# Two layers on one core: attention scores held one head to a PSUM bank, and expert gates spread by transfers

## Chip, cores and metric

One core of a Trainium2 chip runs the whole program. The metric is the device time in microseconds (us) of one execution; before the change it is 1755.88 us, the median of three runs (1743.19 to 1758.93).

The engines are named as in the profile: PE multiplies matrices (PEld is its weight load), DVE is the vector engine, ACT evaluates functions, POOL is the third elementwise engine, SP issues most transfers. PE writes to PSUM, here eight banks of 128 partitions by 512 float32 each. DVE and ACT read the banks and so free them.

## What is computed

2048 tokens of width 128 pass through two layers, each with two parts that are added to the residual stream x:

```python
x = x + ssd(layernorm(x))                  # layer 0: state-space mixer, 8 heads, state 16
h = layernorm(x)                           # layer 0, second part
h1 = h + causal_attention(layernorm(h))    # 16 heads of width 8, all 2048 keys
x = x + h1 + experts(layernorm(h1))        # 8 experts of 128 x 512 x 128, the best 2 gated
x = x + scan(layernorm(x))                 # layer 1: selective scan, 256 channels, state 16
x = x + feed(layernorm(x))                 # layer 1: 128 -> 512 -> 512 -> 512 -> 128

# the attention
scores = where(causal, q @ k.T / sqrt(8), lowest)     # per head, 2048 x 2048
out = softmax(scores) @ v
# the experts
moe_out = sum(gate[:, e] * (gelu(x @ fc1[e] + b1[e]) @ fc2[e] + b2[e]) for e in range(8))
```

## The kernel before

**Tiles.** The tokens are four chunks c of 512 (C). Every part works on a chunk: `ssd(c)`, `prepare(c)` (layernorm, q, k and v), the attention of the chunk, `conclude(c)`, `experts(c)`, `scan(c)`, `feed(c)`. The 16 heads are four groups g of four heads, and the four heads of a group lie on four partition strips of 32, so a score product of one head uses one strip of 32 rows of PE ("32*128" in the profile). The pair (c, g) is one job of the attention, 16 in all.

**The attention of a job has two passes.** `shift(c, g)` (lines 287 to 325) finds for every query the largest score: for each 128 queries r and each chunk of keys kc it multiplies q by k (line 302) for two heads into the two banks of one tile `ps_m`, adds the causal mask with a 128 x 128 product where the keys are the chunk's own (line 311), and one DVE reduction takes the maximum of both heads (line 312). Its result `sh` is laid out at lines 316 to 324. `weighted(c, g)` (lines 327 to 384) goes over the 128-key blocks kb: for two heads at a time it multiplies k by q (line 352) into the two banks of one tile `ps_e`, adds the shift of each query by a second product (line 358), adds the mask on the diagonal (line 360), and one ACT exponential of both heads writes `probs` (line 362). `sum_up` (lines 334 to 342) then multiplies the values by `probs` of all four heads into `ps_o` (line 339, four products on four strips of columns, "128*9"). It is called for block kb - 1 after the first pair of block kb, and the first two of the four products are made to wait for the last exponential of their block as well. A score tile is 2 banks deep and has one buffer, so the next pair's line 302 waits for line 312, and the next pair's line 352 waits for line 362.

**What sets the order.** All parts are Python generators which yield the cost of what they have just written. `in_step` writes a step of `weighted(c, g)` beside steps of `shift` of the next job; `with_attention` writes so much attention between two yields of the other parts (`state_spaces` first, then `second_layers`) as RATE says. The layer above then orders the instructions of each engine by their readiness and by this written order, and puts in the semaphores. Each engine runs its own list strictly in order. After the attention has ended, `scan(2)` with `experts(3)`, `scan(3)` with `feed(2)`, and `feed(3)` alone make up the tail (lines 973 to 978).

**Banks.** `BUFS` at line 81 deals the eight: `m` one tile of two banks, `e` one tile of two banks, `o` one, `a` two, `c` one. The other parts take `a` for their products and `c` for their sums (`Stream`, lines 657 to 688); `ssd` takes `a` and `c` while attention runs beside it. In the tail the stream `other` turns round `m` and `e` and sums in `o` (line 974). The helper `whole` (line 141) hands out half of an `m` or `e` tile where a part asks for one bank.

**Gates.** `experts` (lines 722 to 804) computes the gate of each token and expert, transposes them to rows in `gT` (lines 757 to 774, with a second product that splits them in two halves of precision), and for each expert one product with a selecting weight (`spread_row`, line 719) writes the expert's row to all 128 partitions of a bank; line 785 copies it to `gb`, and line 796 multiplies the expert's output by it. The scan spreads its rows of B in another way: they are written to a DRAM scratch (line 840) and read back to all partitions, one row a transfer of 256 KB (line 861, `bb`).

## Time and profile before

| | us |
|---|---|
| median of three runs (lowest, highest) | 1755.88 (1743.19, 1758.93) |
| the profiled execution | 1741.55 |
| its span, first to last instruction | 1739.8 |
| PE busy, by the page | 1466.9 |
| DVE busy, ACT busy | 975.0, 726.2 |
| mean granted PE clock | 0.837 of full |
| `ssd(0)` alone | about 0 to 140 |
| attention beside the other parts | about 140 to 1410 |
| tail | about 1410 to 1740 |

The page gives busy time by engine, the span in 40 slices (busy tenths, and in the row PEclk the granted PE clock in tenths), and groups of instructions with their count, their busy time and the mean of one. Busy time of a group is the time in which at least one of its instructions ran, so that 640 products of 0.52 us which run two or four abreast are busy for less than their sum. "Idle before" is the engine's idle time just before instructions of the group, with what ended it. The waits view sums the same by who waited for whom. The timeline lists instructions by their start.

### The profile page before, as it was taken

Reading aid. Unit: us, or ns where it says so; the run is one execution under the profiler, and the core shown is the slowest. Engines: PE = TensorE matmul, PEld = TensorE weight load, DVE = VectorE, ACT = ScalarE, POOL = GpSimd, SP = SyncE. Lnnn points to the kernel's source line nnn. Section 1 sums busy time; section 2 is a strip of 40 time slices with the busy share of each in tenths; the row PEclk is TensorE's granted clock in tenths of the full one; section 3 lists DMA queues with packets and bytes.
Section 4 is the critical chain, followed back from the end, with each engine's and each line's share of the span. In section 5 each row is a group of like instructions: output and inputs, shape, how many; then the busy total and the mean of one; then the engine's idle time right before and its main releaser. Section 6 shows DMA issues by size and latency. Waiting matters only on the chain. (4 is left out here: it accounts for less than half of the span.)

```text
span 1739.8 us, 16427 instructions
## 1 busy us (share of the span) xinstructions
PE 1466.9 (84%) x6306; PEld 633.5 (36%) x6306; DVE 975.0 (56%) x1556; ACT 726.2 (42%) x847; POOL 284.0 (16%) x316
## 2 busy tenths in 40 slices
PE   6898999998999888888978887789999888658528
PEld 3554545444333333232333322433333233223214
DVE  4566646557344565667466686674442036774950
ACT  2222322322445444555354454355563536534522
POOL 3322210211000100112111021110000001440220
PEclk9898997887899978889677898669996899868859
DMA  2000000001000000324220045320011022860841
GB/s 85 1 1 1 1 1 1 1 1 55 24 25 25 25 13 21 83 49 103 55 49 14 30 99 107 68 42 25 24 37 31 24 67 78 178 125 31 188 96 30
DMA packets 62494, 83.24 MB, mean 48 GB/s; under 512 B 4576, under 2 KB 28816, under 8 KB 62416
## 3 DMA queue, kind: packets, MB, share of 16 engines
q0 software_dynamic: 16320, 31.46, 10.4%
q1 hardware_dynamic: 45664, 49.68, 9.7%
q8 instruction: 49, 0.80, 0.2%
q10 hardware_dynamic: 432, 1.06, 0.2%
q14 instruction: 29, 0.24, 0.0%
HBM read 49.55 MB, written 1.18 MB: 29 GB/s over the span
## 5 line engine op out<-in xcount | busy, mean ns | idle before, releaser
L362 ACT ACTIVATE probs<-ps_e 128x1024 f32<-128x1024 f32 (+3 forms) x320 | 286.6, 896 | 505.8 <-PE ps_e L358 304.0
L312 DVE TENSOR_REDUCE top<-ps_m 128x2 f32<-128x1024 f32 (+3 forms) x320 | 339.7, 1062 | 280.8 <-PE ps_m L302 164.1
L302 PE MATMUL ps_m<-kR,qR 32*128 32x512 f32 (+3 forms) x640 | 190.1, 523 | 68.0 <-DVE top L312 55.2
L352 PE MATMUL ps_e<-qR,kR 32*128 32x512 f32 (+3 forms) x640 | 175.5, 519 | 27.5 <-ACT probs L362 26.8
L339 PE MATMUL ps_o<-probs,vv 128*9 128x512 f32 (+3 forms) x1152 | 169.7, 599 | 1.0 <-ACT probs L362 0.9
L302 PEld LDWEIGHTS ps_m<-kR,qR 32*128 32x128 f32 x640 | 78.6, 208 | 242.9 <-DVE top L312 132.1
L867 DVE TENSOR_TENSOR_SCAN db<-da,hlast,db 128x512 f32<-128x512 f32 x128 | 163.0, 1310 | 6.5 <-ACT da L863 4.7
L358 PE MATMUL ps_e<-sh,onesR 32*128 32x512 f32 (+3 forms) x640 | 148.9, 431 | 0.0
L352 PEld LDWEIGHTS ps_e<-qR,kR 32*128 32x128 f32 x640 | 69.7, 204 | 182.0 <-ACT probs L362 106.3
L789 PE MATMUL ps_a<-nT,wide 128*128 128x512 f32 x192 | 113.8, 699 | 6.0 <-ACT h L790 3.7
L794 PE MATMUL ps_c<-h,wide 128*128 128x512 f32 x192 | 103.5, 643 | 0.0
L798 POOL TENSOR_TENSOR acc<-acc,ye 128x512 f32<-128x512 f32 x28 | 43.6, 1558 | 331.5 <-DVE ye L796 331.5
L871 POOL COPY hlast<-db 128x2 f32<-128x2 f32 x48 | 29.4, 612 | 378.9 <-DVE db L867 378.9
L863 ACT ACTIVATE da<-dl 128x1024 f32<-128x1024 f32 x64 | 66.4, 1054 | 51.5 <-DMA db<-db 28.3
L865 DVE TENSOR_TENSOR db<-du,bb 128x1024 f32<-128x1024 f32 x64 | 77.9, 1227 | 16.3 <-issue 11.0
L790 ACT ACTIVATE h<-ps_a,cols 128x512 f32<-128x512 f32 x96 | 63.8, 686 | 52.2 <-PE ps_a L789 51.9
L358 PEld LDWEIGHTS ps_e<-sh,onesR 32*128 32x128 f32 x640 | 77.2, 219 | 3.2 <-issue 1.8
L927 PE MATMUL ps_a<-g,wide 128*128 128x512 f32 x96 | 54.0, 690 | 19.5 <-ACT g L930 19.5
L789 PEld LDWEIGHTS ps_a<-nT,wide 128*128 128x128 f32 x192 | 37.1, 215 | 46.3 <-issue 19.5
L362 ACT ACT_TABLE_LOAD x41 | 52.6, 1283 | 1.3 <-PE ps_e L358 0.6
L927 PE MATMUL ps_a<-h,wide 128*128 128x512 f32 x96 | 51.1, 665 | 0.8 <-ACT g L930 0.8
L375 DVE COPY os<-ps_o 128x512 f32<-128x512 f32 x16 | 10.9, 684 | 70.8 <-PE ps_o L339 70.7
(375 smaller groups left out, 2129.3 us busy)
## 6 DMA issues: line engine op xcount, KB each, us to landing
wide<-in_fc SPq DMA_DIRECT2D x64, 256.0 KB, 3.2
bb<-scratch_b SPq DMA_DIRECT2D x64, 256.0 KB, 3.5
db<-db POOLq DMA_DIRECT2D x32, 512.0 KB, 5.7
u<-db POOLq DMA_DIRECT2D x28, 512.0 KB, 6.0
wide<-in_h SPq DMA_DIRECT2D x16, 512.0 KB, 3.7
wide<-in_w SPq DMA_DIRECT2D x8, 256.0 KB, 3.1
x<-in_x SPq DMA_DIRECT2D x4, 256.0 KB, 5.1
w<-in_w SPq DMA_DIRECT2D x4, 256.0 KB, 4.0
```

The source lines that it names most:

```text
L302: nc.tensor.matmul(pss[:, j, 0:n], qR[hr, w - P : w], kR[hr, g, kc * C : kc * C + n], start=True, stop=not diag,)
L312: nc.vector.tensor_reduce(top[:, i : i + 2, kc], pss[:, :, 0:n], AX.X, ALU.max)
L339: pv = nc.tensor.matmul(o, v, prs[i // 2][:, i % 2, q0:], start=kb == 0, stop=kb == nk - 1)
L352: nc.tensor.matmul(pss[:, j, q0:], kR[hr, g, kb * P : (kb + 1) * P], qR[hr, q0:], start=True, stop=False)
L358: nc.tensor.matmul(pss[:, j, q0:], onesR[hr], sh[hr, q0:], start=False, stop=not diag)
L362: last = nc.scalar.activation(pr[:, :, q0:], pss[:, :, q0:], AF.Exp, scale=float(1.0 / np.sqrt(np.float32(HD))))
L789: nc.tensor.matmul(ph, we[:, 0, f * P : (f + 1) * P], nT, start=True, stop=True)
L794: nc.tensor.matmul(py, we[:, 1, f * P : (f + 1) * P], hs[f // 2][:, f % 2, :], start=f == 0, stop=f == NF - 1)
L863: in_turn("exp", nc.scalar.activation(da, dl, AF.Exp, scale=-float(n + 1)))
L865: nc.vector.tensor_tensor(db, du, bb.unsqueeze(1).to_broadcast(two), ALU.mult)
L867: nc.vector.tensor_tensor_scan(db[:, j, :], da[:, j, :], db[:, j, :], hlast[:, j, n : n + 1], ALU.mult, ALU.add)
L927: nc.tensor.matmul(ph, w[k // 2][:, k % 2, f * P : (f + 1) * P], h[k // 2][:, k % 2, :], start=k == 0, stop=k == NF - 1)
```

## The change

One head's scores take one bank. `m` has two buffers of one bank, `e` three; `c` is gone, and what used it takes `a` or the tags listed below. `shift` goes head by head in the order 2, 3, 0, 1. In `weighted`, head i's scores are written and the head is kept in `begun`; at the next head, `finish` adds its shift and mask and issues its exponential just before the next head's scores are written. `probs` remains a tile of two heads. `sum_up` of block kb - 1 comes after the second head of block kb. The gates are transposed once, written to a DRAM scratch and read back, one row a transfer to 128 partitions, in SP's queue. B is no longer held twice (48 rows become 32). The diff, cut to its core:

```diff
-    BUFS = {"m": 1, "e": 1, "o": 1, "a": 2, "c": 1}
+    BUFS = {"m": 2, "e": 3, "o": 1, "a": 2}
...
# prepare: q and k
-                pf = psum("m" if n == "k" else "e", [P, 2, C])
                 for j in range(2):
-                    nc.tensor.matmul(pf[:, j], w[:, g + j], nT, start=True, stop=True)
+                    pf = psum("m" if n == "k" else "e", [P, C])
+                    nc.tensor.matmul(pf, w[:, g + j], nT, start=True, stop=True)
...
# shift
-                for i in (2, 0):
-                    pss = psum("m", [P, 2, C])
-                    for j in range(2):
-                        hr = slice(32 * (i + j), 32 * (i + j) + 32)
-                        nc.tensor.matmul(
-                            pss[:, j, 0:n],
-                            qR[hr, w - P : w],
-                            kR[hr, g, kc * C : kc * C + n],
-                            start=True,
-                            stop=not diag,
-                        )
+                for i in (2, 3, 0, 1):
+                    hr = slice(32 * i, 32 * i + 32)
+                    pss = psum("m", [P, C])
+                    nc.tensor.matmul(
+                        pss[:, 0:n], qR[hr, w - P : w], kR[hr, g, kc * C : kc * C + n], start=True, stop=not diag
+                    )
                     yield None
-                    for j in range(2 * diag):
-                        nc.tensor.matmul(pss[:, j, w - P : w], ident16, mask_qk, start=False, stop=True)
-                    nc.vector.tensor_reduce(top[:, i : i + 2, kc], pss[:, :, 0:n], AX.X, ALU.max)
-                    yield 0.4
+                    if diag:
+                        nc.tensor.matmul(pss[:, w - P : w], ident16, mask_qk, start=False, stop=True)
+                    nc.vector.tensor_reduce(top[:, i, kc : kc + 1], pss[:, 0:n], AX.X, ALU.max)
+                    yield 0.2
...
# weighted
+        def finish(kb, diag, q0, i, pss, pr):
+            hr = slice(32 * i, 32 * i + 32)
+            nc.tensor.matmul(pss[:, q0:], onesR[hr], sh[hr, q0:], start=False, stop=not diag)
+            if diag:
+                nc.tensor.matmul(pss[:, q0 : q0 + P], ident16, mask_kq, start=False, stop=True)
+            last = nc.scalar.activation(
+                pr[:, i % 2, q0:], pss[:, q0:], AF.Exp, scale=float(1.0 / np.sqrt(np.float32(HD)))
+            )
+            return in_turn("exp", last)
+
+        begun = None
...
-            for i in range(0, 4, 2):
-                pss = psum("e", [P, 2, C])
...
+            for i in range(4):
+                hr = slice(32 * i, 32 * i + 32)
+                if i % 2 == 0:
+                    prs.append(ak.tile([P, 2, C], F32, tag="probs", name="probs", bufs=3))
+
+                if begun:
+                    last = finish(*begun)
+                pss = psum("e", [P, C])
+                nc.tensor.matmul(pss[:, q0:], kR[hr, g, kb * P : (kb + 1) * P], qR[hr, q0:], start=True, stop=False)
+                begun = (kb, diag, q0, i, pss, prs[-1])
                 yield None
-                if i == 0 and waiting:
+                if i == 0 and kb:
+                    waiting.append((kb - 1, q_before, prs_before, last))
+                if i == 1 and waiting:
                     sum_up(*waiting.pop())
-                yield 1.1
-            waiting.append((kb, q0, prs, last))
-        sum_up(*waiting.pop())
+                yield 0.55
+            q_before, prs_before = q0, prs
+        last = finish(*begun)
+        sum_up(nk - 1, q0, prs, last)
...
# ssd alone, then ssd beside attention
-        bigs, smalls = ["a", "a", "e"], ["c", "o", "m"]
+        bigs, smalls = ["a", "a", "e", "e"], ["o", "m", "e", "m"]
...
-        bigs[:], smalls[:] = ["a"], ["c"]
+        bigs[:], smalls[:] = ["a"], ["a"]
...
-    side = Stream("", wk, 4, 6, ("a",), "c")
-    scans = Stream("s", wk, 8, 4, ("a",), "c")
+    side = Stream("", wk, 4, 6, ("a",), "a")
+    scans = Stream("s", wk, 8, 4, ("a",), "a")
...
# experts
-        for i in range(2):
-            nc.vector.tensor_tensor(ge2[:, :, i], ge, top.unsqueeze(2).to_broadcast([P, NB, NE]), ALU.mult)
-        pgt = z.bank([2 * NE, C])
...
-        nc.tensor.matmul(pgt, minus_low[NE], ghi, start=False, stop=True, skip_group_check=True)
-        nc.vector.tensor_copy(gT[0 : 2 * NE], pgt)
+        nc.vector.tensor_tensor(ge, ge, top.unsqueeze(2).to_broadcast([P, NB, NE]), ALU.mult)
+        pgt = z.bank([NE, C])
+        for b in range(NB):
+            nc.tensor.transpose(pgt[:, b * P : (b + 1) * P], ge[:, b], ident)
+        gT = z.line("gT", (NE, C))
+        nc.vector.tensor_copy(gT, pgt)
+        gates = scratch_g[c % 2]
+        nc.sync.dma_start(gates, gT)
...
-            pg = z.bank([P, C])
-            spread_row(pg, NE, gT, e)
             gb = z.line("gb")
-            nc.vector.tensor_copy(gb, pg)
+            nc.sync.dma_start(gb, gates[e].partition_broadcast(P))
...
# the tail
-        other = Stream("o", pool, 6, 8, ("m", "e"), "o")
+        other = Stream("o", pool, 6, 8, ("m", "e", "m", "e", "e"), "o")
```

## The prediction on record

> **What bounds the kernel now.** I read the page first: busy times and the slices.
>
> ```profile
> PE 1466.9 (84%) x6306; PEld 633.5 (36%) x6306; DVE 975.0 (56%) x1556; ACT 726.2 (42%) x847; POOL 284.0 (16%) x316
> PE   6898999998999888888978887789999888658528
> PEclk9898997887899978889677898669996899868859
> ```
>
> PE is the fullest engine until the tail, and for long stretches its clock is below full. DVE and ACT have room. So the sum below is one over PE: what it streams, and what it stands still for. Next the page's groups of the attention.
>
> ```profile
> L362 ACT ACTIVATE probs<-ps_e 128x1024 f32<-128x1024 f32 (+3 forms) x320 | 286.6, 896 | 505.8 <-PE ps_e L358 304.0
> L312 DVE TENSOR_REDUCE top<-ps_m 128x2 f32<-128x1024 f32 (+3 forms) x320 | 339.7, 1062 | 280.8 <-PE ps_m L302 164.1
> L302 PE MATMUL ps_m<-kR,qR 32*128 32x512 f32 (+3 forms) x640 | 190.1, 523 | 68.0 <-DVE top L312 55.2
> L352 PE MATMUL ps_e<-qR,kR 32*128 32x512 f32 (+3 forms) x640 | 175.5, 519 | 27.5 <-ACT probs L362 26.8
> ```
>
> 640 products of 0.52 us are busy for only 190 us: heads on different strips run abreast. Then the timeline, in a stretch with no other part beside the attention (the first three lines), and in one with masks (the last four):
>
> ```profile
> 1021.34 0.39 PE L358 MATMUL ps_e<-sh,onesR 32*128 32x512 f32 x2
> 1021.83 1.02 ACT L362 ACTIVATE probs<-ps_e 128x1024 f32<-128x1024 f32 x1 [0.88 <-PE ps_e L358]
> 1022.90 0.51 PE L352 MATMUL ps_e<-qR,kR 32*128 32x512 f32 x2
> ...
> 559.53 0.29 PE L311 MATMUL ps_m<-mask_qk,ident 128*128 128x128 bf16 x2
> 559.75 0.38 PE L352 MATMUL ps_e<-qR,kR 32*128 32x256 f32 x1
> 559.75 0.49 PE L358 MATMUL ps_e<-sh,onesR 32*128 32x256 f32 x2
> 560.18 0.28 PE L360 MATMUL ps_e<-mask_kq,ident 128*128 128x128 bf16 x2
> ```
>
> The first lines are a closed loop. Line 352 starts at 1021.00 (its line is not copied), the shift on the same strips 0.34 later, the exponential 0.49 after that; it takes 1.02, and the next pair's line 352 starts at 1022.90: 1.90 us a pair, while PE streams 0.33 + 0.32, and half of line 339's 0.86 (four strips abreast): 1.09. The rest is the single buffer. Since a record of 0.50 is followed on its strips after 0.33, 0.17 of a record is drain. With that taken off each PE record, the idle time ahead of lines 302 and 352 in the whole trace is 155 us; by the page's records (68.0 + 27.5) it is 95.5.
>
> **Part 1, more buffers: -100 us.** Softmax: three banks, each held for 0.33 + 0.49 + an exponential of 512 columns (0.60, the row of line 362 in the view by shapes) + 0.1, so a head each 0.5 us; ACT itself needs 0.60. Maxima: a reduction of 512 columns is 0.69 in that view, so DVE paces a pair at 1.38, with its semaphore 1.45. The stall of a pair falls from 1.90 - 1.09 = 0.81 to 0.36, by 56%: 155 x 0.56 = 87. Line 320, 378 and 165 and the first line 302 after a job, which wait for the one `ps_m` (12 us for `sh`, about 10 for the others), gain some 13. Ends: -130 (hardly a stall left) and -60 (in-order PE waits for DVE's other work as before).
>
> **Part 2, the masks: +115 us.** A mask is a product over all 128 rows, between products of 32. In pairs, two shifts, two masks and two scores each stand together. Now the mask of one head comes between its shift and the next head's scores, and these two no longer run abreast on the diagonal. Spacings at full clock from the timeline: shift to mask 0.32 at 512 columns (0.26, 0.21, 0.15 at 384, 256, 128; mean 0.23); scores to shift 0.335, mean 0.25; mask to mask 0.056; mask to a 32-row product 0.15 (the last mask at 559.60, line 352 at 559.75). Before, a pair is 0.25 + 0.23 + 0.06 + 0.15 = 0.69, or 0.34 a head; after, 0.23 + 0.15 + 0.25 = 0.63. With 256 diagonal heads (the count of line 360): 0.29 x 256 = 74. In `shift` a mask now costs per head scores to mask 0.425 in place of 0.335, and 0.15 back: 0.24 x 256 = 61, against about 0.16 a pair, 20. Together 115 at full clock, 137 at the mean 0.837; I leave about a fifth under reductions that PE would have waited for. Ends +60 and +140.
>
> Here a rule of the Trainium skill speaks against the change: TensorEngine Tiling (Array Packing), Key Properties, says that changing the tiling mode, not just the tile, drains TensorE. The trace has this at 0.09 us: scores to mask 0.425 against scores to shift 0.335, mask to scores 0.15 against mask to mask 0.056. A whole drain of 0.17 at each of some 1000 changes would add 80 us; the sum uses the 0.09.
>
> **Part 3, line 339's wait: +25.** `sum_up` needs the exponential of the last head, now issued one step before it: shift + 0.49 + 0.60 = 1.09 us. If PE paces the steps, line 339 is reached about 0.7 after that shift and waits 0.4 on 160 blocks: 64, and the next shift and scores, which stand behind it in PE's queue, are late too, and with them ACT. If DVE paces, it waits near nothing. The page has 1.0 us for line 339 now. I take 25.
>
> **Part 4, fixed costs of ACT and DVE: +10.** Exponentials: 448 x 0.597 + 64 each of 0.49, 0.38 and 0.28 = 341 for 287. Reductions: 448 x 0.69 + 64 x (0.55 + 0.42 + 0.29) = 388 for 340. The covers are PE's work (DVE 56% busy); where DVE is at three quarters and more (750 to 800, 1000 to 1050, 1100 to 1150) some 47 pairs pay 0.16 each: 8. Without cover it would be about 50.
>
> **Part 5, `c` gone: +8.** Expert sums (3.4 us of products, then line 796 of 0.75), the scan's and the feed's sums now sit in one of two `a` banks. Attention between two yields hides most; if each of some 40 sums held PE up for its 0.75, 30.
>
> **Part 6, gates: -20.** What goes:
>
> ```profile
> L785 DVE COPY gb<-ps_a 128x512 f32<-128x512 f32 x24 | 16.3, 679 | 2.1 <-PE ps_a L719 2.1
> L719 PE MATMUL ps_a<-rows_in,two_rows 128*128 128x512 f32 x24 | 14.0, 584 | 0.2 <-DVE rows_in L774 0.2
> bb<-scratch_b SPq DMA_DIRECT2D x64, 256.0 KB, 3.5
> ```
>
> 32 products of 0.41 (0.58 less drain): 13 of PE, 22 of DVE, and in the tail 19 us in which PE waits for `gb` with two banks in turn. There the scan sets the end, so I count 5; and 2 for the shorter transpose. What comes: four writes of 16 KB and 32 reads like `bb` in SP's queue, 3.5 us to landing and wanted only after the expert's first products. SP's queue is in order: a gate read that waits for a free line (POOL's sum of the expert before) holds the weights and the scan's `bb` behind it. SP already waits 355 us for line 865 to free `bb`, so it runs ahead; if that cover were gone, 16 steps of `scan(0)` could each lose up to 3.5 us beside `experts(1)`: at most 56. The five banks of the tail and two more of the start give 3.
>
> **Part 7, the clock: 0, ends -60 and +40.** The trace in windows of 3.4 us (busy times of the engines, then PEclk):
>
> ```profile
> 515.90:519.30 3.40, 1.25 (x10) 0.49 (x10) 2.19 (x3) 1.35 (x2) 0.00 (x0) 1.00 0.00 0
> 519.30:522.70 3.40, 2.72 (x8) 0.75 (x8) 1.85 (x2) 2.01 (x3) 0.00 (x0) 0.50 0.00 0
> 526.10:529.50 3.40, 3.40 (x9) 1.52 (x8) 0.00 (x0) 0.51 (x1) 0.00 (x0) 0.50 0.00 0
> 529.50:533.00 3.50, 3.50 (x15) 1.25 (x13) 1.01 (x3) 2.93 (x4) 0.00 (x0) 0.99 0.00 0
> ```
>
> PE busy for 1.25 of 3.4 us halves the clock; a full window brings it back. The page TensorE: Matmul & The Clock Gate of the Trainium skill (Why this matters for your kernels) puts the drop at idle gaps of over about 3 us. By that rule nothing here would throttle (the longest gap ahead of a score product is under 4 us, and few are over 2) and this part is 0 for certain; by the trace, short stalls that fill half a window suffice. A mean of 0.837 is half clock for a third of the span, so fewer stalls could give back tens of us; new ones (part 3) would take them. I put 0 in the sum.
>
> **The sum.** -100 + 115 + 25 + 10 + 8 - 20 - 3 = +35. The profiled execution took 1741.6 (span 1739.8 and 1.8 around it), so 1777; the median of the runs shown is 14.3 above it: **1791 us**, 2% slower.
>
> **The rivals.**
> - *The stalls were the dearer part* (27%): masks fall where PE would wait for a reduction anyway. -110 + 65 + 0 + 5 + 3 - 23, and the clock gives 20: -80, so 1676. For it: the idle time is there, and it lowers the clock. Against it: each diagonal head costs PE 0.63, near DVE's 0.69, so little hides. It decides below about 60 us of mask cost with line 339 waiting for nothing.
> - *Gain and cost cancel* (15%): 1756.
> - *New waits add up in PE's queue* (15%): line 339 waits its full 64 (+39), the two `a` banks cost 30 (+22), the clock another 25: +121, so 1877. For it: PE is in order and every one of these stands ahead of the scores.
> - *It doesn't do what it says*: the layer that orders the instructions need not put a shift beside the next head's scores. If a quarter of the 640 heads lost that, 160 x 0.33 = 53 us; this is within the range.
>
> **Chances.** Forecast 43% (own range 1760 to 1825), the rivals 27, 15 and 15. About 1% is what a measurement of this kernel can tell from no change (1738 to 1773). Faster 0.27; same 0.15; slower 0.58. Range: 1675 to 1870, which leaves out about half of the first and of the third rival.
>
> **What would show it.** Idle ahead of lines 302 and 352 should fall from 95.5 by records to under 50; PE's busy time rise by about 100; the rows of the masks be followed by score products at 0.15; line 339 show idle time ended by `probs`; `gb` land long before line 796. I am wrong if PE's busy time doesn't rise, or if the mean clock moves by over 0.03.

## The result and the profile after

| | us |
|---|---|
| before, beside the new kernel (lowest, highest of 4) | 1756.6 (1743.19, 1758.93) |
| after, median of 4 (lowest, highest) | 1874.03 (1867.70, 1893.36) |
| ratio, 95% interval | 1.070 [1.062, 1.078] |
| the profiled execution, its span | 1867.7, 1866.0 |
| mean granted PE clock | 0.819 |
| `ssd` ends, attention ends (before: 419, 1419) | 532, 1544 |

Slower by 7%, and just above the range. Below, ratios leave out slow runs, those over 1.5% above the fastest of their kernel; medians are over all runs. 113 of the 126 us between the two spans are lost by the time the last `ssd` ends (532 for 419). By then both kernels have done the same part of the attention (123 and 124 of the 640 score products of the softmax), most of it on the diagonal; the tail is the same to 1 us. The page of the kernel after, rows of its first two parts:

```profile
PE 1669.2 (89%) x6254; PEld 746.8 (40%) x6254; DVE 985.2 (53%) x1832; ACT 747.6 (40%) x1161; POOL 276.1 (15%) x315
...
PE   6899999999999999999999899999999999636638
...
PEclk8786677587779998778877878868999999866869
```

PE has 52 instructions fewer than before, is busy 202 us longer, and by its records hardly stands still until the tail. DVE and ACT have 10 and 21 us more. So I looked for the loss on PE itself. In slices 4 to 12 PE is at 9 tenths throughout, and its clock at 5 to 8. The page's groups of the attention, and the shifts of before, whose row was not shown:

```profile
L302 DVE TENSOR_REDUCE top<-ps_m 128x1 f32<-128x512 f32 (+3 forms) x640 | 377.2, 607 | 323.1 <-PE ps_m L301 155.3
L296 PE MATMUL ps_m<-kR,qR 32*128 32x512 f32 (+3 forms) x640 | 314.7, 531 | 19.1 <-DVE top L302 15.1
L357 PE MATMUL ps_e<-qR,kR 32*128 32x512 f32 (+3 forms) x640 | 274.4, 519 | 21.2 <-ACT probs L339 19.8
L336 PE MATMUL ps_e<-sh,onesR 32*128 32x512 f32 (+3 forms) x640 | 247.7, 459 | 0.6 <-DVE sh L314 0.4
L329 PE MATMUL ps_o<-probs,vv 128*9 128x512 f32 (+3 forms) x1152 | 191.4, 603 | 3.2 <-ACT probs L339 2.6
...
L358 PE MATMUL ps_e<-sh,onesR 32*128 32x512 f32 (+3 forms) x640 | 148.9, 431 | 0.0
```

The change does what it says: the idle time ahead of the score products is 40.3 by records, for 95.5. But the same 640 products of the same length are busy for 314.7 and 274.4 us, where they took 190.1 and 175.5, and the shifts take 247.7 for 148.9. The mean of one score product hardly moved (531 and 519 ns for 523 and 519). Busy time of a group is the time in which at least one of its instructions runs, so fewer of its products overlap. The timeline shows one way in which they come apart (PE only, softmax on the diagonal):

```profile
1201.16 0.50 PE L336 MATMUL ps_e<-sh,onesR 32*128 32x512 f32 x1
1201.59 0.23 PE L338 MATMUL ps_e<-mask_kq,ident 128*128 128x128 bf16 x1
1201.75 0.50 PE L357 MATMUL ps_e<-qR,kR 32*128 32x512 f32 x1
1201.75 0.50 PE L296 MATMUL ps_m<-kR,qR 32*128 32x512 f32 x1
1202.09 0.39 PE L336 MATMUL ps_e<-sh,onesR 32*128 32x512 f32 x1
1202.42 0.23 PE L338 MATMUL ps_e<-mask_kq,ident 128*128 128x128 bf16 x1
```

From the first mask to the second is 0.83 us (0.16 from mask to scores, 0.34 to the next shift, 0.33 to the next mask), and in the 0.33 one strip of 32 rows works and three do nothing. The stretch from 300 to 400 us, in after and then in before (columns: busy us of PE, PEld, DVE, ACT, POOL with their counts, then the granted clock, and the DMA's share and GB/s):

```profile
300.00:400.00 100.00, 97.81 (x350) 53.87 (x350) 44.39 (x100) 17.88 (x39) 9.39 (x11) 0.61 0.00 0
...
300.00:400.00 100.00, 93.33 (x490) 44.93 (x488) 57.02 (x111) 32.51 (x43) 18.94 (x21) 0.81 0.00 1
```

PE is busy for 97.81 of 100 us and gets 0.61 of its clock, where before it was busy for 93.33 and got 0.81. Idle time does not account for the lower clock here.

I counted both traces in one way, from 140 us to the end of the attention: 0.17 us of drain is taken off each PE record, and each moment goes to the first of these that runs: a product over all rows of other parts, the values' product, 32-row products by how many strips are at work, a mask alone, nothing. In brackets the same with the half-clock time counted half, that is, at full clock.

| us | one strip alone | two | three | four | masks | values | all rows | nothing | at half clock |
|---|---|---|---|---|---|---|---|---|---|
| before | 30 (24) | 186 (155) | 12 (10) | 43 (31) | 32 (27) | 171 (138) | 529 (446) | 278 (236) | 430 |
| after | 218 (177) | 102 (84) | 49 (39) | 16 (12) | 37 (30) | 187 (149) | 541 (440) | 255 (226) | 502 |

At full clock the 32-row products take 92 us more, masks 3, values 11, all rows 6 less, standing still 10 less: +90. Half of the 72 us more at half clock are 36. Together 126, against 125 between the two ends of the attention; the count has to close, so it says where the time went and not why. The runs' own spans and clocks give the same split with less chance in it: span times granted clock (the time at full clock) is 1529 us over the four runs of after and 1452 over 14 of before, and the rest, lost to the clock, 347 and 302. That is +77 and +45. I use this working again below.

### The profile page after: what moved, and what is told of

Its sections match the earlier page's. It is cut to its first block, busy times and chain, and to the rows that moved or that the text cites. A ratio compares the mean times of both kernels' runs of the same rounds, so it can differ in the third digit from the quotient of the medians.

```text
span 1866.0 us, 17011 instructions
## 1 busy us (share of the span) xinstructions
PE 1669.2 (89%) x6254; PEld 746.8 (40%) x6254; DVE 985.2 (53%) x1832; ACT 747.6 (40%) x1161; POOL 276.1 (15%) x315
## 3 DMA queue, kind: packets, MB, share of 16 engines
HBM read 57.90 MB, written 1.25 MB: 32 GB/s over the span
## 4 chain that ended last, share of the span: by engine, by line
PE 74%; DVE 11%; issue 6%; ACT 5%; DMA 2%; POOL 2%; SPq 0%; POOLq 0%; DVEq 0%; ACTq 0%
PE ps_o L329 10%; PE ps_e L357 8%; PE ps_e L336 7%; PE ps_m L296 6%; PE ps_a L756 6%; PE ps_a L761 5%; DVE db L834 3%; PE ps_a L894 3%; PE ps_m L301 2%; DVE top L302 2%; PE ps_e L338 2%; ACT probs L339 2%; PE ps_a L586 2%; PE ps_a L561 1%; PE ps_a L544 1%
## 5 line engine op out<-in xcount | busy, mean ns | idle before, releaser
L302 DVE TENSOR_REDUCE top<-ps_m 128x1 f32<-128x512 f32 (+3 forms) x640 | 377.2, 607 | 323.1 <-PE ps_m L301 155.3
L339 ACT ACTIVATE probs<-ps_e 128x512 f32<-128x512 f32 (+3 forms) x640 | 317.4, 533 | 553.0 <-PE ps_e L338 296.2
L296 PE MATMUL ps_m<-kR,qR 32*128 32x512 f32 (+3 forms) x640 | 314.7, 531 | 19.1 <-DVE top L302 15.1
L357 PE MATMUL ps_e<-qR,kR 32*128 32x512 f32 (+3 forms) x640 | 274.4, 519 | 21.2 <-ACT probs L339 19.8
L336 PE MATMUL ps_e<-sh,onesR 32*128 32x512 f32 (+3 forms) x640 | 247.7, 459 | 0.6 <-DVE sh L314 0.4
L296 PEld LDWEIGHTS ps_m<-kR,qR 32*128 32x128 f32 x640 | 127.2, 212 | 135.2 <-DVE top L302 79.1
L357 PEld LDWEIGHTS ps_e<-qR,kR 32*128 32x128 f32 x640 | 111.5, 204 | 125.4 <-ACT probs L339 62.5
L761 PE MATMUL ps_a<-h,wide 128*128 128x512 f32 x192 | 102.1, 643 | 0.0
L301 PE MATMUL ps_m<-mask_qk,ident 128*128 128x128 bf16 x256 | 62.9, 246 | 0.0
L338 PE MATMUL ps_e<-mask_kq,ident 128*128 128x128 bf16 x256 | 62.1, 243 | 0.0
```

The source lines that it names most:

```text
L296: nc.tensor.matmul(pss[:, 0:n], qR[hr, w - P : w], kR[hr, g, kc * C : kc * C + n], start=True, stop=not diag)
L301: nc.tensor.matmul(pss[:, w - P : w], ident16, mask_qk, start=False, stop=True)
L302: nc.vector.tensor_reduce(top[:, i, kc : kc + 1], pss[:, 0:n], AX.X, ALU.max)
L336: nc.tensor.matmul(pss[:, q0:], onesR[hr], sh[hr, q0:], start=False, stop=not diag)
L338: nc.tensor.matmul(pss[:, q0 : q0 + P], ident16, mask_kq, start=False, stop=True)
L339: last = nc.scalar.activation(pr[:, i % 2, q0:], pss[:, q0:], AF.Exp, scale=float(1.0 / np.sqrt(np.float32(HD))))
```

## The experiments

Three theories at the start. **A**: the masks between the 32-row products are the cost, and more than forecast. **B**: the bank `c` is, through sums that wait for `a`. **C**: products of single heads stand less abreast whether there are masks or not. Each kernel is compared with before on the same chip.

| kernel | median us | ratio to before [95%] |
|---|---|---|
| before_nomask | 1741.87 | 0.991 [0.988, 0.994] |
| after_nomask | 1714.84 | 0.977 [0.970, 0.984] |
| after_maskmove | 1861.32 | 1.058 [1.053, 1.063] |
| no_c_alone | 1786.54 | 1.016 [1.010, 1.023] |
| gates_alone | 1728.55 | 0.988 [0.982, 0.994] |
| after_nomaxmask | 1846.08 | 1.045 [1.035, 1.055] |
| after_poolmask | 1753.35 | 1.001 [0.999, 1.004] |
| after_c_back | 1971.06 | 1.123 [1.115, 1.131] |
| masks_behind | 1785.32 | 1.020 [1.013, 1.027] |
| masks_behind_nomax | 1756.11 | 1.000 [0.997, 1.003] |
| poolmask_later | 1742.78 | 0.994 [0.992, 0.996] |
| pair_maxima | 1920.29 | 1.089 [1.079, 1.098] |
| pair_softmax | 2004.02 | 1.141 [1.136, 1.147] |
| gates_nomaxmask | 1727.46 | 0.983 [0.978, 0.989] |
| maxima_twos | 1795.44 | 1.025 [1.016, 1.034] |
| both_twos | 1729.59 | 0.987 [0.979, 0.995] |
| maxima_twos_nomask | 1769.37 | 1.010 [1.007, 1.013] |

**The masks out of both kernels** (before_nomask, after_nomask). In each, both lines of masks go, so a query also sees later keys of its own chunk. The edit of after:

```diff
-                    if diag:
-                        nc.tensor.matmul(pss[:, w - P : w], ident16, mask_qk, start=False, stop=True)
...
-            nc.tensor.matmul(pss[:, q0:], onesR[hr], sh[hr, q0:], start=False, stop=not diag)
-            if diag:
-                nc.tensor.matmul(pss[:, q0 : q0 + P], ident16, mask_kq, start=False, stop=True)
+            nc.tensor.matmul(pss[:, q0:], onesR[hr], sh[hr, q0:], start=False, stop=True)
```

> The kernel before without either causal mask product (lines 311 and 360 left out, so the attention also sees later keys of its own chunk). Theory A (masks between products of 32 rows make the change slow): before, the masks stand in pairs and cost little, some 40 us of PE work at most: 1715 to 1745 against 1757. Theory B (the bank c that is gone makes it slow) and theory C (single-head pieces run less abreast whatever the masks do) say the same of this run; it is the base for the next one.

> The kernel after without either causal mask product. Theory A: nearly all of the 117 us goes: within 30 us of the run of before without masks. Theory B: the masks don't matter for the difference: still about 100 us above before without masks, and the stage of ssd beside attention still some 100 us longer than before's. Theory C: a good half remains, 50 to 90 us, and the busy time of the 32-row products stays near 380 us (drain taken off) instead of near 270.

The masks cost the kernel before 13 us (1755.05 on this chip less 1741.87) and the kernel after 159: 146 more for the same 512 products. Without them the change gains 27. So A holds as to where the loss sits, and C as it was put (50 to 90 us left) falls. But C isn't nothing: in my count for after_nomask one strip works alone for 147 us (125 at full clock) against 25 (21) in before_nomask, and the 32-row products at full clock take 264 for 216, so 48 us of such work are added with no mask in sight.

**The softmax's mask behind the next head's scores** (after_maskmove).

```diff
                 if begun:
-                    last = finish(*begun)
+                    shifted(*begun)
                 pss = psum("e", [P, C])
                 nc.tensor.matmul(pss[:, q0:], kR[hr, g, kb * P : (kb + 1) * P], qR[hr, q0:], start=True, stop=False)
+                if begun:
+                    last = finish(*begun)
```

> The kernel after with the softmax's mask of a head written behind the next head's scores, so that a shift and the next scores stand side by side on the diagonal too; the mask product itself stays. Theory A by the prediction's own working: 256 diagonal heads save one of two narrow spacings of 0.25 us at full clock, 64 us, and the clock comes back in part: 1780 to 1815 against 1874. Theory B: 1860 to 1875. Theory C: a small gain, 1840 to 1865.

A miss for A as I had put it (1780 to 1815): 13 us. The time lies in the ranges that the text gave to B and C. The shift and the next scores are abreast now, but the maxima's score, which had been beside those scores, stands alone: still two groups of 32-row products a head (one strip alone for 192 us, 218 before this edit).

**The bank c alone, and the gates alone.** no_c_alone is the kernel before with `c` out of `BUFS` and its users on `a` (and one stream shorter at the start); gates_alone is the kernel before with the gates' part of the change.

> The kernel before with the bank c taken away alone: ssd's small products beside attention and the sums of side and scans go to a, as after; scores stay in pairs, gates stay as they are, one bank lies idle. Theory A and theory C: the prediction's part 5, +8 us with ends 0 and 30: 1757 to 1787. Theory B: 1830 to 1870, with the stage of ssd beside attention about 100 us longer.

> The kernel before with the gates spread by transfers alone; scores in pairs and the bank c as before. The prediction's part 6: -20 us, 1725 to 1745 against 1755. The rival theory (a gate read waits for a free line in SP's queue and holds weights and B rows behind it): 1770 to 1810, with idle time of DVE or PE ended by the transfers gb, bb or wide.

In the kernel before the bank is worth 31 us, and in the trace without it PE stands still for some 35 us more at full clock. That is far from the 1830 to 1870 of B. What the bank is worth among the new banks no run measures alone. The gates gain 23.

**One mask fewer, the masks on POOL, and the third softmax bank.** after_nomaxmask takes line 301 out. after_poolmask has no mask product; after the exponentials of two heads POOL sets the probabilities above the diagonal to zero. after_c_back deals `{"m": 2, "e": 2, "o": 1, "a": 2, "c": 1}`.

> The kernel after without the mask of the maxima alone (line 301 left out). The maximum is then taken over the later keys of the own block too; a softmax does not change with its shift, so this leaves out no part of the result. Both masks together cost 159 us in the kernel after. If the cost is one per change of tiling mode, each mask has about half of it: 1785 to 1805. If it is the shift and the scores that the softmax's mask parts (the prediction's reason), the maxima's mask has the lesser part, some 45 us: 1820 to 1835.

> The kernel after without either mask product; the probabilities of later keys are set to zero on POOL after the exponential (128 selections of 128 x 256, about 0.4 us each by the selections at the start of the trace), so the softmax is masked as in the reference. If the mask products alone made the change slow, this is near the kernel after without masks, 1715 to 1735. If the way over POOL makes line 329 late, 1740 to 1780.

> The kernel after with two banks for the softmax in place of three, and the bank c back for the sums and for ssd's small products. Taking c away from the kernel before cost 31 us. If that adds up, 1835 to 1850; if the third softmax bank is worth as much, 1865 to 1885.

The maxima's mask alone accounts for 28 of the 159 by medians and for some 44 by the ratios (1.045 for 1.070), the figure of its text's second case. POOL in place of both gives 121 back, but not all: in its trace line 341 on POOL takes 0.49 us 128 times, and values' products wait for it:

```profile
L327 PE MATMUL ps_o<-probs,vv 128*9 128x512 f32 (+3 forms) x1152 | 178.3, 589 | 23.9 <-POOL probs L341 19.4 <-ACT probs L335 4.0
```

A softmax in single heads with two banks is 97 us worse than with three, although `c` is back.

**Three abreast, masks together** (masks_behind, masks_behind_nomax). Of a head, only the shift is written with the next scores; its mask and exponential come one `yield None` later, so that the maxima's step lies between:

```diff
-                    last = finish(*begun)
+                    shifted(*begun)
...
-                begun = (kb, diag, q0, i, pss, prs[-1])
+                ended, begun = begun, (kb, diag, q0, i, pss, prs[-1])
                 yield None
+                if ended:
+                    last = finish(*ended)
```

> The kernel after, with a head's softmax mask and exponential written one step later: a head's shift, the next head's scores and a maxima's scores then come one behind the other on three strips, and the two masks of a step (softmax's and maxima's) stand together behind them. The number of masks and of mode changes per head hardly moves. Theory A1 (the masks cost so much because they part the three 32-row products of a step into two groups of which each takes its own 0.25): on 256 diagonal heads one group less, 0.25 to 0.4 each, 64 to 100 us less at full clock, and the clock rises: 1765 to 1800. Theory A2 (the switch to the mask and back, and the time that the banks are held longer, are the cost): little changes, 1840 to 1865. Theory C (the third softmax bank is what the loop lives on): the exponential comes a step later, so every bank is held longer, and the time gets worse than after: 1880 to 1930.

> The same as masks_behind, without the mask of the maxima (the maximum is then one over all columns of the block, which only changes the shift that the softmax divides out). A1: one mask a head, behind three products abreast: 1735 to 1780. A2: near the kernel without the maxima mask alone, 1825 to 1850. C: over 1850.

89 us back from writing the same instructions in another order, with no mask fewer and the exponential later: in my count one strip alone falls from 218 to 164 us, and half clock from 502 to 406. Its timeline, at half clock (products of 512 columns last 0.79 here):

```profile
1120.62 0.29 PE L340 MATMUL ps_e<-mask_kq,ident 128*128 128x128 bf16 x1
1120.84 0.68 PE L336 MATMUL ps_e<-sh,onesR 32*128 32x384 f32 x1
1120.85 0.68 PE L359 MATMUL ps_e<-qR,kR 32*128 32x384 f32 x1
1120.85 0.79 PE L296 MATMUL ps_m<-kR,qR 32*128 32x512 f32 x1
1121.57 0.29 PE L340 MATMUL ps_e<-mask_kq,ident 128*128 128x128 bf16 x1
```

One group of three between two masks. The number of masks is the same, so it is not what the 89 us are. The changes of mode did move, unlike what the text says: by the order of the records, PE changes between 32-row products and others 1538 times in the attention of after and 1325 times here. At the prediction's 0.09 us a change, 213 fewer are an estimated 19 of the 89 us, and after_nomaxmask has fewer still (1298), with half the masks, for half the gain by the ratios. So A2 falls as the larger cost: it is that a mask parts the products. That the exponential comes later did not make it worse (the C of that text falls). Leaving out the maxima's mask as well gains 29 more.

**POOL's masks with more cover** (poolmask_later): `sum_up` after the third head, four buffers of `probs`.

> The kernel after with no mask product at all: the maxima are taken over all columns, and POOL sets the probabilities above the diagonal to zero once for two heads. Unlike the earlier kernel of this kind (1753) the product of probabilities and values is written after the third head of the next block in place of the second, with one more buffer of probabilities, so that POOL's 0.49 and the wait ahead of it lie beside other work. If the 27 us that PE waited for POOL's result, and the exponentials queued behind it, are what separates that kernel from the one without masks (1715): 1715 to 1735. If POOL's [...]queue is what costs: 1750 again.

11 us back of 39; part of POOL's price, and between the two figures that I gave.

**What lowers the clock** (clock_blocks).

```diff
+        all_rows(200); rows_32(300, 1)
+        all_rows(200); rows_32(300, 2)
+        all_rows(200); rows_32(300, 3)
+        all_rows(200); rows_32(300, 4)
+        for n in range(240):
+            rows_32(1, 1)
+            nc.tensor.matmul(banks[0][:, 0:P], ident16, mask_qk, start=True, stop=True)
```

> The kernel before with blocks of products appended at its end, each in one unbroken row on PE, on data that is already there and with nothing read from them: 300 products of 32 rows on one strip, 300 pairs on two strips, 300 triples on three, 300 quadruples on four, then 240 times a product of 32 rows and one of 128x128 in 16 bits (a mask), with 200 products over all 128 rows ahead of each. It has extra work, so only the granted clock of each block is read. Theory of the idle gaps: PE never stands still, so the clock is full in every block. Theory of the used rows: one strip alone brings the clock to half although PE is busy throughout, four strips keep it full, and two and three lie between; strip and mask by turns is at half.

`rows_32(n, s)` writes n rounds of one product on each of s strips, `all_rows(n)` n products over all rows. Windows of the one execution, in order: all rows, one strip, all rows, two strips, three strips, four strips, and strip and mask by turns, from 5.3 us after this block began:

```profile
1742.00:1789.30 47.30, 47.26 (x201) 38.70 (x201) 0.00 (x0) 0.00 (x0) 0.00 (x0) 0.96 0.02 6
1789.30:1912.80 123.50, 123.50 (x302) 93.82 (x301) 0.00 (x0) 0.00 (x0) 0.00 (x0) 0.52 0.00 0
1912.80:1960.60 47.80, 47.80 (x201) 39.08 (x200) 0.00 (x0) 0.00 (x0) 0.00 (x0) 0.95 0.00 1
1960.60:2028.90 68.30, 68.30 (x602) 60.13 (x601) 0.00 (x0) 0.00 (x0) 0.00 (x0) 1.00 0.01 1
...
2074.40:2142.70 68.30, 68.30 (x902) 60.16 (x901) 0.00 (x0) 0.00 (x0) 0.00 (x0) 1.00 0.01 2
...
2188.20:2256.50 68.30, 68.30 (x1202) 60.33 (x1201) 0.00 (x0) 0.00 (x0) 0.00 (x0) 1.00 0.01 2
...
2262.00:2340.00 78.00, 78.00 (x169) 32.01 (x168) 0.00 (x0) 0.00 (x0) 0.00 (x0) 0.50 0.00 0
```

PE is busy all but without a gap in each. One strip alone runs at half clock: 300 products in 123.5 us. Two strips do 600 products, three 900, four 1200, in 68.3 at full clock, each after a block that had it at full clock. A strip and a mask by turns, which is part of what a diagonal head does in the kernel after, is at half clock. So idle gaps are not the only thing that lowers the clock.

The kernel's traces say more. The clock's changes lie on a grid of 3.4 us. I weighted each moment of such a window by the strips of 32 rows at work (a product over all rows as four, drain taken off). In after, 53 of 346 windows at full clock are followed by half clock, and they are those with a weight under 0.43 of all four strips: this line puts 19 of the 346 on the wrong side, while the best line by PE's busy share puts 39 there. At half clock the return takes a weight of 0.83 (16 of 198 wrong). In nine traces that I worked so the two lines lie at 0.41 to 0.46 and 0.80 to 0.85; in before, where lone strips are few, the busy share tells the drops nearly as well (23 wrong of 341, for 21). Between the two lines the clock stays what it was: the groups of three of masks_behind above are at half clock, and nothing there brings it back.

**One half of the change at a time** (pair_maxima: maxima again in pairs, softmax single; pair_softmax: before with the gates and single maxima in two banks), **and gates_nomaxmask**, gates_alone without line 311.

> The kernel after with the maxima in pairs again (one buffer of two banks): the softmax in single heads, the missing ninth kind of bank and the gates remain. If the softmax's mask between the shift and the next head's scores is the dear part, as the forecast had it (74 of 115): most of the loss stays, 1810 to 1850. If the maxima's single heads are (their scores standing alone between two masks): 1750 to 1790.

> The kernel before with the gates by transfers and the maxima alone in single heads in two banks, the small sums in their own bank: only the maxima's half of the change beside a gain of 23 for the gates. By the forecast's terms for the maxima (about 41 for the masks, 4 for the reductions, some 40 to 50 gained by the second buffer): near the gates alone, 1720 to 1745. If single-head maxima are the dear part: 1780 to 1830.

> The kernel before with the gates by transfers and no mask in the maxima (the maximum is then over all columns of the block, which only moves the shift that the softmax divides out). If masks in pairs cost little, as the kernel before without any masks says (14 for both): within 10 us of the gates alone, 1718 to 1730. If the mask of the maxima holds DVE's reduction up: 1705 to 1718.

(The missing "ninth kind of bank" of these texts is `c`.) Both halves missed, and neither text had it: each half alone is slower than the whole change. The parts don't add up; the maxima alone cost 275 over gates_alone. My first reading was that single scores had at least stood beside each other (see the timeline of after), while a single score beside pairs doesn't find company. But one strip works alone for 227 us in pair_softmax and 207 in pair_maxima, for 218 in after. What grew is half clock: 826 and 591 us, for 502. By the runs' spans and clocks the time at full clock is 1519, 1546 and, for after_c_back, 1530 us, for 1529 in after; 488, 364 and 436 are lost to the clock, for 347. So what pair_softmax and after_c_back take over after is the clock, and in pair_maxima half of it is. The next kernels ask what the order of writing does to it.

**Single banks, but written in twos** (maxima_twos from pair_softmax; both_twos from after; maxima_twos_nomask, which leaves out the maxima's mask). For the maxima:

```diff
-                for i in (2, 3, 0, 1):
-                    hr = slice(32 * i, 32 * i + 32)
-                    pss = psum("m", [P, C])
-                    nc.tensor.matmul(
+                for i in (2, 0):
+                    two = []
+                    for j in range(2):
+                        hr = slice(32 * (i + j), 32 * (i + j) + 32)
+                        pss = psum("m", [P, C])
+                        nc.tensor.matmul(
...
+                        two.append(pss)
                     yield None
-                    if diag:
+                    for pss in two[: 2 * diag]:
                         nc.tensor.matmul(pss[:, w - P : w], ident16, mask_qk, start=False, stop=True)
```

and the reductions of the two behind; both_twos does the same in the softmax, with `sum_up` where before had it.

> pair_softmax (2004: softmax in pairs, maxima in two single banks) with one thing changed: two heads of the maxima are written together, scores, scores, then both masks, then the two reductions, each into its own bank. Banks, reductions and products are the same in number. If what makes that kernel slow is that a maxima's score stands alone on its strip: back to 1725 to 1780, and the time in which one strip works alone falls from 227 us toward the 26 of the gates alone. If it is the 640 single reductions or the two separate banks: 1950 to 2010. Between, where the two banks come free one by one and the ordering by readiness parts the two products again.

> The kernel after with both passes written in twos as before (scores of two heads, then two shifts, two masks), but with its banks: single ones, two for the maxima and three for the softmax, no ninth kind, single reductions and exponentials, gates by transfers. It has the change's buffers without its order of writing. By lone strips: near 1730 to 1790 if the twos stay together. If separate banks part the twos by readiness: 1800 to 1900, with a time of one strip alone over 100 us.

> maxima_twos without the mask of the maxima (the maximum over all columns of the block only moves the shift that the softmax divides out). Near gates_nomaxmask (1727) if the twos stay together; above it by as much as maxima_twos is above the gates alone otherwise.

209 us back by order alone, with the same banks and the same 640 reductions; by spans and clocks some 64 at full clock and 150 of the clock. The page's groups of pair_softmax:

```profile
L304 DVE TENSOR_REDUCE top<-ps_m 128x1 f32<-128x512 f32 (+3 forms) x640 | 381.2, 608 | 251.8 <-PE ps_m L303 133.8
L298 PE MATMUL ps_m<-kR,qR 32*128 32x512 f32 (+3 forms) x640 | 359.7, 618 | 36.1 <-DVE top L304 30.9
```

and of maxima_twos:

```profile
L308 DVE TENSOR_REDUCE top<-ps_m 128x1 f32<-128x512 f32 (+3 forms) x640 | 370.1, 605 | 281.4 <-PE ps_m L300 158.0
L300 PE MATMUL ps_m<-kR,qR 32*128 32x512 f32 (+3 forms) x640 | 276.3, 540 | 41.4 <-DVE top L308 35.4
```

DVE is busy 11 us less and PE waits 5 us more for it; the scores are busy 83 us less, one strip alone falls from 227 to 121 us, and half clock from 826 to 498. That it is 67 above gates_alone is in its text's middle case: the trace has 121 us of one strip still, for 26. Two banks that come free one by one let the ordering by readiness part the two products again, as I read it; with a tile of two banks both wait for the same buffer. Without the maxima's mask the same distance is 42 (1769.37 for 1727.46), so masks are not all of it.

both_twos, with all of the change's banks, is 144 us faster than after, and faster than before:

```profile
L298 PE MATMUL ps_m<-kR,qR 32*128 32x512 f32 (+3 forms) x640 | 264.3, 523 | 36.6 <-DVE top L306 31.1
L347 PE MATMUL ps_e<-qR,kR 32*128 32x512 f32 (+3 forms) x640 | 220.7, 510 | 7.4 <-ACT probs L357 6.5
L352 PE MATMUL ps_e<-sh,onesR 32*128 32x512 f32 (+3 forms) x640 | 188.4, 438 | 0.1
```

These three sum to 673.4 busy us, 836.8 in after, 514.5 before. Nothing runs for 200 us at full clock (236 before), the 32-row products take 269 (220), one strip alone 159 us: the finer banks do save stalls, and more 32-row work takes that back. Its time is in the range for twos that stay together, but its 159 us of one strip is the mark that the text gave to the other case: the twos come apart in part, and still half clock is 393 us for 502 in after. Of the 144 us, about half is at full clock and half is the clock (71 and 77 by spans and clocks). The edit also moves `sum_up` and the exponentials back, which no run parts from the order of the products. It is no faster than the gates alone. Both it and the gates alone beat both kernels, before by just over 1%; gates_nomaxmask (1727.46) adds nothing that can be measured.

## Why the prediction was wrong

The sign was right, the size was not: +35 forecast, +117 measured. Two routes give the same split in number. Masks taken out of both kernels: 146 for the masks, -27 for the rest. The order in twos kept (both_twos): 144 for the order, -26 for the rest. The forecast had +115 and -80, so 53 of the miss is in the rest and some 30 in the masks. Both routes start from the same before and after; that they agree to 2 us is in part luck, as the parts of the change need not add up (pair_maxima, pair_softmax).

- **Part 1 is the step that failed.** It wrote a pair as 1.09 of PE's streaming and 0.81 of stall, and let only the stall shrink. The 1.09 holds while two heads stream for the price of one. In single heads they do so less, on the diagonal or off it: 48 us more of 32-row work at full clock without any mask, counted at nothing. The stalls ahead of score products shrank, from 155 to 106 us (87 forecast, 49 measured), but ahead of shifts, masks and values' products they grew from some 44 to 105. Standing still in all fell by 10 at full clock. If the parts did add up, with 31 for `c` and -23 for the gates some -40 would be left for this part's -100, an estimate. The line that I read, idle ahead of lines 302 and 352, came out as forecast (under 50) and said nothing of this.
- **Part 2 had the right mechanism and the right spacings, but not the right sum.** It wrote 0.32 + 0.15 + 0.335 for a head of 512 columns; the timeline above has 0.33 + 0.16 + 0.34. At full clock in my counts the masks cost 58 more than before (1153 with and 1064 without in after, 1064 and 1033 in before), half of its 115. What makes 146 of it is the clock: in after 502 us run at half clock with the masks and 379 without, so 61 us more for them; in before the masks cost no clock at all (430 with, 505 without). Spans and clocks of all runs agree: of the 146, 57 at full clock and 87 of the clock. And the pair that it saw parted, a shift and the next scores, was worth only 13 us by itself (after_maskmove); it took all three products abreast to gain 89.
- **Part 7 put the clock at 0** and looked for its cause in stalls that fill half a window. The window that it read (PE busy for 1.25 of 3.4) fits that, but stalls aren't the only cause: in clock_blocks one strip with no gap is at half. No line that it showed could have told this, as none had a strip alone. The mean moved only from 0.837 to 0.819, inside my 0.03, and yet it is 36 us by half-clock time, or 45 by all the runs (0.828 to 0.815): the bound of 0.03 was too wide to be a sign. Kernels with the same attention differ by some 30 us of half-clock time between profiles (399 to 430 for before, gates_alone and no_c_alone), so 36 is good to some 15. The rule that it cited, from the Trainium skill's page TensorE: Matmul & The Clock Gate (Why this matters for your kernels), ties the drop to idle gaps of over about 3 us; where it and clock_blocks differ, the measurement decides. From 140 us to the end of the attention, before has 35 stretches at half clock and four idle gaps of PE over 3 us by records (3.2 to 3.6), so the rule gives few of them. Three of the four are ahead of score products, so "nothing here would throttle" did not follow from it either.
- **Part 3**: line 329 waits 3.2 us by records, 24.8 for 19.4 with the drain taken off. +5, not +25.
- **Part 4**: the reductions take 37 us more (48 forecast) and the exponentials 31 (54 forecast), DVE and ACT in all +10 and +21; no run measures what this costs.
- **Part 5**: 31 by no_c_alone, not 8; it lies just above the upper end of 30. The attention between two yields covers less than I took it to.
- **Part 6**: -23 for the gates by themselves, -20 forecast. `gb` lands in 3.7 us.
- **PE's busy time** was to rise by about 100 and rose by 202: the first figure of the page that shows the miss. Some of it is the clock, since a record at half clock is longer.
- **The rival of new waits** came closest in time (1877), by luck: the values' products wait for 3.2 us by records where it had 64, and PE as a whole stands still no longer than before. The rival that the ordering parts the shift from the next scores named the right quantity, abreast or not; that its 53 us is near the 48 that single heads cost without masks is chance, as it left the masks and the clock out.

Open: why the clock falls further with half of the change than with the whole. That it does is measured, for pair_softmax without more time of a lone strip than in after, and that order alone gives 209 us of it back is shown; which products missed each other in pair_maxima, and why its values' products take more, I did not separate. How much of POOL's remaining 28 us over after_nomask is its latency and how much its queue is open as well.

## What to carry to other kernels

Products on a quarter of the rows were cheap here only in company: before a buffer is split in two, ask what kept their instructions side by side, for it may have been the shared buffer. Judge a change to such code by how many strips work at once and by half-clock time, not by the stalls ahead of the products. And a full-width product written between narrow ones cost what it parted, more than what it took: write it behind the group.

## What the runs showed of the hardware

- The clock falls with PE busy throughout, when one strip of 32 rows is at work or a strip and a 128x128 mask by turns (0.52 and 0.50); two strips abreast kept 1.00 where the clock was full when they began. The drop came 5.5 us after the lone strip's block began, and the return 4.8 us after the next block, over all rows, did.
- In windows of 3.4 us, weighted by the strips at work, the line for a drop lies at 0.41 to 0.46 of all rows and that for a return at 0.80 to 0.85 (nine traces, each line with 4 to 10% of the windows on the wrong side). These are fits to my count, not settings that I could read.
- Two, three and four strips with 512 columns took 0.228 us a round at full clock (68.3 for 300), and one strip alone 0.41 at half clock (123.5 for 300): one alone takes 1.8 times as long as up to four together.
